# Last block of a conditioned residual chain: another order of W1's terms, x3T made from the transposed normalized values, and extra TensorE products

## The chip, the cores and the metric

The kernel runs on one core of a Trainium2 chip. The metric is the device time of one execution in microseconds (us), the median of three runs. One further execution was recorded by the hardware profiler; the profile and the trace are of that one. Engines are named as in the profile: PE is TensorE, DVE is VectorE, ACT is ScalarE, POOL is GpSimd, and SP is SyncE, whose queue starts most of the DMAs.

## The reference

The input is x, 128 sequences of 64 tokens with 256 features, and a condition vector of 128 numbers per sequence. Four layers are added to it, one after the other:

```python
x = x + L0(x, cond_512)        # attention with modulated projections
x = x + L1(x, cond_512)        # small adapter, weights made per sequence
x = x + L2(x, ids, cond_512, cond_64, fside)
x = x + L3(x, cond_512)        # linear layer, weights made per sequence
```

The change concerns the end of L2 and the beginning of L3. Cut to what matters:

```python
# L2: h, t, s are layer norms of x with gains and biases looked up by token ids,
#     m, n, r are x plus one vector per sequence; w = softmax(aw)
cat = concatenate([w0*h, w1*t, w2*m, w3*n, w4*r, w5*s])
y   = silu(cat @ W1 + b1) @ W2 + b2
L2  = (y - mean(y)) * rsqrt(var(y) + 1e-5) * g + be
# L3: U is made from mu per sequence, V is shared
weight, bias = U[:, :-1, :] @ V, U[:, -1, :] @ V
L3  = x @ weight + bias
```

## The kernel before, in words

The 8192 tokens are worked in 16 blocks of 512 tokens (8 sequences), a block in 4 tiles of 128 tokens. A prologue loads weights and derives tables that all blocks use. Each block runs `attention` (L0) and then `rest` (L1, L2, L3). Most values are kept with features on the partitions: x1T is x after L0, x2T after L1, x3T after L2, each 2 x 128 partitions by 512 tokens (index c for the half). For the layer norms x2T is turned to tokens on the partitions (x2, four tiles).

Steps of `rest` in order, with their lines:

- x2T is made by DVE at L1217, from the L1 products at L1204. PE transposes it (L1254), ACT copies the tiles out as x2 (L1257), and DVE takes their statistics (L451, L452).
- The normalized tiles xn (L1240) are multiplied by and added to gathered rows on POOL (L1265, L1271), which gives h; h is normalized again (L1240).
- xn and h are transposed (L1289) and copied out (L1292). Products with a one-hot matrix (L1298) give the gains by token, and DVE multiplies them in (L1307). The results are g, xnT and hnT.
- W1 is a sum of four terms in one PSUM bank for each half of the output (L1322): `w_t` by g, `w_x` by x2T, `w_s` by xnT, `w_h` by hnT. A last product (L1331) adds the biases. Each term takes two products of 128x512, in f32, and shows as four records a half. ACT and DVE make s2 of it (L1337, L1340).
- W2 (L1353) gives y by tile; DVE adds a bias (L1358) and takes the statistics mvy. POOL derives the factor ry and the offset nry (L456, L458, L1234, L1235; the power at L458 is the long one).
- ACT normalizes the four tiles (L1240). POOL multiplies each by the gain (L1364) and adds x2 (L1367): that is x3. PE transposes x3 (L1379); ACT adds the bias in the transposed layout (L1384): that is x3T.
- L3 is PE at L1396 (x3T by U), DVE at L1407 (zT), PE at L1422 (zT by V). DVE adds x3 (L1430) and SP stores (L1434), tile by tile.

The order of the instructions is not the order of this text. Every operation is recorded in a list with the buffers that it reads, writes or claims. The class `Plan` then orders all of them by a list schedule on the host, with its own costs for every engine (`pe(us, ...)`, `act`, `dve`, `pool`), its own idea of PE's clock, and a table of priorities, `TURNS`, one number for each operation of a block. There is one table for each of "prologue", "first", "second", "middle", "last but one" and "last"; where several operations can start at once on an engine, the lowest number goes first. Each engine then runs its instructions in this fixed order and waits with semaphores. Buffers are handed out by kind. There are four PSUM buffers of the kind "bank". There is one buffer of the kind "s2", which s2 and x3T take in turn. The first product of W1 claims it for its block, so that W1 of a block begins after the block before has read its x3T.

`early` is a constant of many columns that is loaded at the start; `lbe` is L2's bias `be` in it, one number per partition, and `lg` is the gain `g` repeated on all partitions.

Of the kernel before, what the change touches and what calls it, by code (L numbers as in the profile page):

```python
# [42 lines left out]
EARLY_WIDTHS = (B, 8, C, 2, 2, 1, C, C, C, 1, 6) + (C,) * 9  # L43
# [15 lines left out]
class Plan:  # L59
# [44 lines left out]
    def stream(self, t, work, full):  # L104

        now, left = t, work
        while left > 1e-9:
            n = int(now / self.WINDOW)
            speed = 1.0 if n and self.cells.get(n - 1, 0.0) >= self.BUSY else 0.5
            m = int((now + self.SEEN) / self.WINDOW)  # L110
            step = max(min((n + 1) * self.WINDOW, (m + 1) * self.WINDOW - self.SEEN) - now, 1e-6)
            step = min(step, left / speed)
            self.cells[m] = self.cells.get(m, 0.0) + step * speed * full / self.WINDOW
            left -= step * speed
            now += step
        return now - t

# [101 lines left out]
    -10633 41137 464 10909 -44878 -11608 -42604 -45090 10155 -44468  # L219
# [14 lines left out]
    -15193 -45201 -12582 9703 17987 22744 15597 -18168 17424 -28042 -41758 -7357 -451 25437 -8991 -12614 459 -11776  # L234
    29958 -7569 23567 -6641 13097 26814 -28106 7375 -575 12318 20069 -38198 23459 -38462 36836 27311 31943 -4776
    26854 -14776 2811 12753 3636 -20535 28655 16056 22892 -31515 6510 -3096 -41775 12301
# [14 lines left out]
    1457 -45077 -25320 -34934 -8032 -37786 -19094 -8437 5339 -12394 -20304 14994 3721 -11664 -7635 -27664 27176 20895  # L251
    26121 9336 -35791 -14043 -7673 8369 -42327 -31969 -25693 17291 2553 -36411 -3402 -15873 13422 7027 -32778 19435
    22712 -20010 12141 -39669 -37660 1149 -27222 -44023 37623 -37115 -18717 26495 3505 18710 -32292 -430 15236 18791
    21609 -17410 29738
# [13 lines left out]
    28780 21150 7584 9227 29132 5260 28987 31520 -2237 3828 8090 938 30118 3864 -4871 -7133 4057 30319 11418 -2268  # L268
    -597 -6095 7699 -2331 11788 11039 36273 619 1024 4669 34043 16725 5303 33221 -6438 31026 14080 11161 37456 23037
    11095 -11007 27922 -5110 11858 21714 35520 -1388 28909 27611 779 30000 -4851 23042  # L270
    """,
    "last but one": """
    -945 -5006 28741 3275 -555 -2679 4333 19756 13246 29462 3507 42603 5115 -1489 14772 22434 -2133 33481 31798 41815
    951 30003 36734 39833 31441 44287 36835 36712 48388 29816 33965 35152 6423 18014 27987 -10794 26523 6071 13375
    215 -9627 40936 -4357 6362 10572 4554 -7283 41533 17559 2437 32059 31798 -2882 16598 41191 820 4323 8748 36137
    -10897 4648 -575 -2079 4645 -3815 1256 27711 36689 35506 -1449 -434 19376 3801 26228 18811 24911 28300 -6303
    26981 -11699 25941 12883 26660 40398 20930 37525 4574 -10903 34299 29604 46591 6477 -4378 -5383 30451 28410 33294
    18120 33105 30216 -4508 44002 39404 3003 11400 29 3543 3766 -5799 -2138 811 18752 32082 3511 3445 11417 27797
    5708 -499 -3099 10586 -5165 8292 24437 31597 33482 -11432 5280 4641 43330 5970 12741 11648 -6313 39403 7099 3725
    -1194 -2199 33524 5684 -3093 -3282 30904 3501 1070 957 -1360 33574 5400 34372 27196 29366 -2640 -4017 6600 27342  # L280
    3755 1799 30520 32280 29029 46575 20997 32367 9369 29333 -3636 1757 5073 38 16950 4247 -3714 31630 -87 5434 33087
    13695 12804 -1538 27383 -6571 45385 6618 32455 18229 25530 13431 4352 28866 4197 42996 36274 28905 48852 20492
    25821 12505 -1402 -5360 3342 27949 30405 6793 33874 -4408 26737 -9042 5014 33335 43087 44838 12803 42849 4251
    28780 21150 7584 9227 29132 5260 28987 31520 -2237 3828 8090 938 30118 3864 -4871 -7133 4057 30319 11418 -2268
    -597 -6095 7699 -2331 11788 11039 36273 619 1024 4669 34043 16725 5303 33221 -6438 31026 14080 11161 37456 23037
    11095 -11007 27922 -5110 11858 21714 35520 -1388 28909 27611 779 30000 -4851 23042
    """,
    "last": """
    -945 -5006 28741 3275 -555 -2679 4333 19756 13246 29462 3507 42603 5115 -1489 14772 22434 -2133 33481 31798 41815
    951 30003 36734 39833 31441 44287 36835 36712 48388 29816 33965 35152 6423 18014 27987 -10794 26523 6071 13375  # L290
    215 -9627 40936 -4357 6362 10572 4554 -7283 41533 17559 2437 32059 31798 -2882 16598 41191 820 4323 8748 36137
    -10897 4648 -575 -2079 4645 -3815 1256 27711 36689 35506 -1449 -434 19376 3801 26228 18811 24911 28300 -6303
    26981 -11699 25941 12883 26660 40398 20930 37525 4574 -10903 34299 29604 46591 6477 -4378 -5383 30451 28410 33294
    18120 33105 30216 -4508 44002 39404 3003 11400 29 3543 3766 -5799 -2138 811 18752 32082 3511 3445 11417 27797
    5708 -499 -3099 10586 -5165 8292 24437 31597 33482 -11432 5280 4641 43330 5970 12741 11648 -6313 39403 7099 3725
    -1194 -2199 33524 5684 -3093 -3282 30904 3501 1070 957 -1360 33574 5400 34372 27196 29366 -2640 -4017 6600 27342
    3755 1799 30520 32280 29029 46575 20997 32367 9369 29333 -3636 1757 5073 38 16950 4247 -3714 31630 -87 5434 33087
    13695 12804 -1538 27383 -6571 45385 6618 32455 18229 25530 13431 4352 28866 4197 42996 36274 28905 48852 20492
    25821 12505 -1402 -5360 3342 27949 30405 6793 33874 -4408 26737 -9042 5014 33335 43087 44838 12803 42849 4251
    28780 21150 7584 9227 29132 5260 28987 31520 -2237 3828 8090 938 30118 3864 -4871 -7133 4057 30319 11418 -2268  # L300
    -597 -6095 7699 -2331 11788 11039 36273 619 1024 4669 34043 16725 5303 33221 -6438 31026 14080 11161 37456 23037
    11095 -11007 27922 -5110 11858 21714 35520 -1388 28909 27611 779 30000 -4851 23042
# [5 lines left out]
def resid_chain(ctx: ExitStack, tc: tile.TileContext, a: dict, out: bass.AP, nblk: int = NBLK):  # L308
# [104 lines left out]
    condT, tok8, kab, apart, hilo, rowid, oab, ob, lbe, bdl, aw, *small = columns("early", EARLY_WIDTHS)  # L413
# [15 lines left out]
    def pe(us, f, reads, writes, claims=(), full=1.0, mode=0):  # L429

        op("PE", us + 0.16, f, reads, writes, busy=us, claims=claims, full=full, mode=mode)

# [740 lines left out]
    def rest(blk, x1T, pw, oh, wdn, wup, tab, uT):  # L1173

        b0 = blk * NB

# [139 lines left out]
        for fc in range(C):  # L1316
            ps, th = Buf("bank"), Buf("tmp")
            for n, (w, src) in enumerate(((w_t, gs), (w_x, x2T), (w_s, xnT), (w_h, hnT))):
                for c in range(C):
                    pe(  # L1320
                        0.88,
                        lambda ps=ps, w=w, src=src, fc=fc, c=c, n=n: nc.tensor.matmul(  # L1322
                            ps.t, w.t[:, c, bass.ts(fc, 128)], src.t[:, c, :], start=(n == 0 and c == 0), stop=False
                        ),
                        [w, (src, c) if src is not x2T else src],
                        [ps],
                        [th, s2],
                    )
# [16 lines left out]
            )  # L1345
        mvy, ry, nry = Buf("mvy"), Buf("ry"), Buf("nry")
        x3 = [Buf("x3") for _ in range(NTILE)]
        for tl in range(NTILE):
            ps = Buf("bank")

            def second(ps=ps, tl=tl):
                for c in range(C):
                    nc.tensor.matmul(  # L1353
                        ps.t[:, :F], s2.t[:, c, bass.ts(tl, 128)], w2.t[:, c, :], start=(c == 0), stop=(c == C - 1)
                    )

            pe(0.88, second, [s2, w2], [ps], [x3[tl]])
            dve(256, lambda ps=ps, tl=tl: nc.vector.tensor_tensor(x3[tl].t, ps.t[:, :F], b2, ALU.add), [ps], [x3[tl]])  # L1358
            stats(x3[tl], mvy, tl)
        rstd(mvy, ry)  # L1360
        offset(mvy, ry, nry)
        for tl in range(NTILE):
            normalize(x3[tl], x3[tl], ry, nry, tl)
            pool(0.65, lambda tl=tl: nc.gpsimd.tensor_tensor(x3[tl].t, x3[tl].t, lg, ALU.mult), [x3[tl]], [x3[tl]])  # L1364
            pool(
                0.65,
                lambda tl=tl: nc.gpsimd.tensor_tensor(x3[tl].t, x3[tl].t, x2[tl].t, ALU.add),  # L1367
                [x3[tl], x2[tl]],
                [x3[tl]],
            )  # L1370
# [3 lines left out]
        for c in range(C):  # L1374
            ps = Buf("bank")

            def turn(ps=ps, c=c):
                for tl in range(NTILE):
                    nc.tensor.transpose(ps.t[:, bass.ts(tl, 128)], x3[tl].t[:, bass.ts(c, 128)], ident)  # L1379

            pe(0.5, turn, x3, [ps], [x3T])
# [66 lines left out]
def _layouts(i):  # L1448
# [32 lines left out]
    for n in ("mem", "noi", "res"):  # L1481
# [49 lines left out]
        + [columns(int_be)]  # L1531
# [28 lines left out]
```

## Time and profile before

| | value |
|---|---|
| runs | 897.14, 897.73, 900.79 us; median 897.73 |
| profiled execution | 896.84 us, its span 895.1 us |
| granted TensorE clock, mean | 0.984 |
| PE busy | 824.6 us (92% of the span) |
| DVE, ACT, POOL busy | 635.5, 446.8, 608.0 us |
| last block: x2T ready | 843.7 us |
| last block: first and last record of W1 | 854.22, 870.6 us |
| last block: nry ready | 878.4 us |
| last block: last addition of L1430 ends | 891.6 us |

The span goes from the first to the last instruction of the profiled execution; what lies around it makes the rest of its time. A chain of waits is followed back from the last instruction, at each step to what released it. Buffers that share memory show under the name of the memory in the trace: "uu", "p" and "bank" stand for several of the names above, so an operation is found by its line.

### The profile page before, as it was taken

Reading aid. Unit: us, or ns where it says so; the run is one execution under the profiler, and the core shown is the slowest. Engines: PE = TensorE matmul, PEld = TensorE weight load, DVE = VectorE, ACT = ScalarE, POOL = GpSimd, SP = SyncE. Lnnn points to the kernel's source line nnn. Section 1 sums busy time; section 2 is a strip of 40 time slices with the busy share of each in tenths; the row PEclk is TensorE's granted clock in tenths of the full one; section 3 lists DMA queues with packets and bytes.
Section 4 is the critical chain, followed back from the end, with each engine's and each line's share of the span. In section 5 each row is a group of like instructions: output and inputs, shape, how many; then the busy total and the mean of one; then the engine's idle time right before and its main releaser. Section 6 shows DMA issues by size and latency. Waiting matters only on the chain.

```text
span 895.1 us, 23962 instructions
## 1 busy us (share of the span) xinstructions
PE 824.6 (92%) x9752; PEld 534.3 (60%) x9752; DVE 635.5 (71%) x1363; ACT 446.8 (50%) x825; POOL 608.0 (68%) x826
## 2 busy tenths in 40 slices
PE   5769999999999999999999999999999999999783
PEld 3548746556665756666566657566665666564442
DVE  2779867868685868777786858787777868585532
ACT  1454453555464655545554645555455556464321
POOL 4464683949687795959495876959594968754423
PEclk9889999999999999999999999999999999999996
DMA  8768742223424232322333332333323322101000
GB/s 252 202 155 239 247 132 76 71 82 108 116 84 122 67 118 81 109 81 76 113 96 117 85 119 70 119 81 94 95 73 116 96 85 83 49 15 59 1 24 25
DMA packets 62575, 90.24 MB, mean 101 GB/s; under 512 B 6328, under 2 KB 46200, under 8 KB 62464
## 3 DMA queue, kind: packets, MB, share of 16 engines
q1 hardware_dynamic: 57344, 71.92, 28.1%
q0 software_dynamic: 5120, 16.78, 5.9%
q8 instruction: 77, 1.26, 0.6%
q14 instruction: 34, 0.28, 0.1%
HBM read 75.44 MB, written 13.24 MB: 99 GB/s over the span
## 4 chain that ended last, share of the span: by engine, by line
PE 44%; POOL 26%; DVE 13%; issue 6%; ACT 6%; DMA 3%; SPq 1%; POOLq 0%; DVEq 0%; ACTq 0%
PE bank L1322 15%; PE sc L1053 4%; DVE mt L1062 4%; PE bank L964 3%; PE bank L1353 3%; PE bank L1128 3%; PE bank L997 3%; POOL kxe L1011 2%; POOL wdn L938 2%; POOL uu L1271 2%; DVE st L451 2%; POOL xsT L907 2%; POOL uu L1265 2%; ACT uu L1240 2%; POOL uu L1364 1%
## 5 line engine op out<-in xcount | busy, mean ns | idle before, releaser
L1117 ACT ACTIVATE e<-sc 128x1024 f32<-128x1024 f32 x128 | 125.9, 1022 | 79.5 <-PE sc L1103 79.5
L1062 DVE TENSOR_REDUCE mt<-sc 128x8 f32<-128x1024 f32 x128 | 151.8, 1205 | 11.8 <-PE sc L1053 8.8
L1147 POOL TENSOR_TENSOR att<-ao,rz 128x256 f32<-128x256 f32 x45 | 28.1, 626 | 71.0 <-DVE rz L1144 66.8
L1307 DVE TENSOR_TENSOR uu<-uu,bank 128x512 f32<-128x512 f32 x96 | 63.8, 680 | 15.5 <-PE bank L1298 14.3
L997 PE MATMUL bank<-wk,xsT 128*128 128x256 f32 x256 | 70.1, 409 | 1.0 <-POOL xsT L907 1.0
L1322 PE MATMUL bank<-uu,w_s 128*128 128x512 f32 x128 | 66.9, 604 | 0.0
L1322 PE MATMUL bank<-uu,w_t 128*128 128x512 f32 x128 | 63.2, 604 | 2.2 <-DVE uu L1307 2.2
L1322 PE MATMUL bank<-x2T,w_x 128*128 128x512 f32 x128 | 64.4, 606 | 0.0
L1353 PE MATMUL bank<-w,uu 128*128 128x256 f32 x256 | 61.4, 383 | 1.0 <-DVE uu L1340 1.0
L456 POOL TENSOR_SCALAR ry<-mvy 128x4 f32<-128x4 f32 (+1 forms) x19 | 4.4, 232 | 85.3 <-DVE mvy L452 85.2
L964 PE MATMUL bank<-osT,wo 128*128 128x512 f32 x128 | 59.3, 604 | 0.5 <-DVE osT L1163 0.5
L997 PEld LDWEIGHTS bank<-wk,xsT 128*128 128x128 f32 x256 | 48.3, 200 | 19.3 <-issue 10.8
L1322 PE MATMUL bank<-uu,w_h 128*128 128x512 f32 x128 | 59.1, 597 | 0.6 <-DVE uu L1307 0.4
L1072 ACT COPY mt<-mt 128x16 f32<-128x16 f32 x64 | 13.1, 204 | 84.0 <-DVE mt L1062 83.9
L451 DVE BATCH_NORM_STATS2 st<-uu 128x6 f32<-128x256 f32 x119 | 48.3, 417 | 8.8 <-ACT uu L1257 4.7
L1011 POOL TENSOR_TENSOR kxe<-kxe,kbr 128x256 f32<-128x256 f32 x64 | 46.8, 731 | 8.7 <-DVE kxe L1005 6.3
L1353 PEld LDWEIGHTS bank<-w,uu 128*128 128x128 f32 x256 | 46.2, 190 | 8.3 <-DVE uu L1340 1.6
L938 POOL TENSOR_TENSOR wdn<-gdb,late 128x512 f32<-128x512 f32 x32 | 40.6, 1273 | 11.6 <-PE bank L1186 6.1
L1005 DVE TENSOR_TENSOR kxe<-bank,dmk 128x256 f32<-128x256 f32 x64 | 26.8, 419 | 29.9 <-PE bank L997 26.8
L922 POOL DMA_INDIRECT pw<-in_pw,idx x39 | 40.0, 1025 | 8.1 <-issue 7.2
L1140 DVE STREAM_TRANSPOSE ao<-bank 128x512 f32<-128x512 f32 x45 | 32.0, 711 | 18.0 <-PE bank L1128 18.0
L952 POOL TENSOR_TENSOR wup<-wup,ubb 128x512 f32<-128x512 f32 x32 | 40.6, 1269 | 3.5 <-DMA ubb<-ugub 1.3
(199 smaller groups left out, 2114.3 us busy)
## 6 DMA issues: line engine op xcount, KB each, us to landing
xT<-in_xT SPq DMA_DIRECT2D x32, 256.0 KB
gdb<-dgdb SPq DMA_DIRECT2D x16, 512.0 KB
ubb<-ugub SPq DMA_DIRECT2D x32, 256.0 KB
wup<-ugub SPq DMA_DIRECT2D x32, 256.0 KB
dmk<-demod_k SPq DMA_DIRECT2D x30, 256.0 KB
out_x<-uu SPq DMA_DIRECT2D x35, 128.0 KB
ud<-uu SPq DMA_DIRECT2D x8, 512.0 KB
uT<-ud SPq DMA_DIRECT2D x16, 256.0 KB
```

The costliest lines, as they stand in the source:

```text
L451: dve(256, lambda: nc.vector.bn_stats(st.t, x.t), [x], [st])
L922: lambda tl=tl, n=n: nc.gpsimd.indirect_dma_start(out=pw[tl].t, out_offset=None, in_=a["pw"], in_offset=bass.IndirectOffsetOnAxis(ap=idx[: ...
L938: lambda w=w, dp=dp: nc.gpsimd.tensor_tensor(w(), gdb.t[:, :, 0:64], dp, ALU.mult),
L952: pool(1.25, lambda w=w: nc.gpsimd.tensor_tensor(w(wup), w(wup), w(ubb), ALU.add), [wup, ubb], [wup])
L964: nc.tensor.matmul(ps.t, owT[:, c, bass.ts(oc, 128)], osT.t[:, c, :], start=(c == 0), stop=(c == C - 1))
L997: nc.tensor.matmul(ps.t[:, :F], xsT.t[:, c, bass.ts(tl, 128)], kwT[:, c, :], start=(c == 0), stop=(c == C - 1))
L1011: lambda: nc.gpsimd.tensor_tensor(kxe.t[:, :, 0:D], kxe.t[:, :, 0:D], heads(kinds["kbr"][0]), ALU.add),
L1062: lambda two=two: nc.vector.tensor_reduce(mt.t[:, two, 0:4], sc.t[:, two, :].rearrange("p q (g n) -> p q g n", g=4), AX.X, ALU.max),
L1117: lambda k=k: nc.scalar.activation(es[k].t, sc.t[:, 2 * k : 2 * k + 2, :], AF.Exp, scale=0.25),
L1307: lambda ps=ps, src=src, dst=dst, c=c: nc.vector.tensor_tensor(dst.t[:, c, :], src.t[:, c, :], ps.t, ALU.mult),
L1322: lambda ps=ps, w=w, src=src, fc=fc, c=c, n=n: nc.tensor.matmul(ps.t, w.t[:, c, bass.ts(fc, 128)], src.t[:, c, :], start=(n == 0 and c == ...
L1353: nc.tensor.matmul(ps.t[:, :F], s2.t[:, c, bass.ts(tl, 128)], w2.t[:, c, :], start=(c == 0), stop=(c == C - 1))
```

## The change

For the last block alone (`quick`), four things differ.

1. W1's terms come in another order: `w_x` by x2T first, then `w_t`, `w_s`, `w_h`.
2. ACT adds `lbe` to x2T in place, after everything else has read x2T. The normalized tiles go to buffers of their own, yn. PE transposes yn instead of x3, and one DVE operation makes x3T: the transposed yn, times the gain `lgT` (one number per partition, two new columns of `early`), plus x2T with its bias. POOL still makes x3 from yn for the final addition.
3. `keep` adds products that nobody reads. Each group starts with a product of four columns whose moving operand is a value just made (mvy, ry, nry, then yn of tiles 0, 1 and 2), and goes on with 4 (for the first three) or 3 products of the identity with itself, 128x128 in f32. They take a PSUM bank and PE's time. The plan books 0.12 us for each.
4. The priority tables "last but one" and "last" are new; in the others, places for the added operations are put in, and other blocks skip them (`skip`). "prologue" has six more numbers, for the six groups.

```diff
-EARLY_WIDTHS = (B, 8, C, 2, 2, 1, C, C, C, 1, 6) + (C,) * 9
+EARLY_WIDTHS = (B, 8, C, 2, 2, 1, C, C, C, C, 1, 6) + (C,) * 9
...
+    def skip(self, n):
+
+        self.noted[self.blk] += n
...
+    def keep(n, gate):
+
+
+        ps, blk = Buf("bank"), plan.blk
+        plan.blk = -1
+
+        def products():
+            nc.tensor.matmul(ps.t[:, :4], ident, gate[1](), start=True, stop=True)
+            for k in range(n):
+                nc.tensor.matmul(ps.t[:, bass.ts(k, 128)], ident, ident, start=True, stop=True)
+
+        pe(0.12 * n, products, [gate[0]], [ps])
+        plan.blk = blk
...
+        quick = blk == nblk - 1
...
-            for n, (w, src) in enumerate(((w_t, gs), (w_x, x2T), (w_s, xnT), (w_h, hnT))):
+            terms = (w_t, gs), (w_x, x2T), (w_s, xnT), (w_h, hnT)
+            if quick:
+                terms = terms[1], terms[0], *terms[2:]
+            for n, (w, src) in enumerate(terms):
...
+        if quick:
+            for c in range(C):
+                act(
+                    512,
+                    lambda c=c: nc.scalar.activation(x2T.t[:, c, :], x2T.t[:, c, :], AF.Identity, bias=lbe[:, c : c + 1]),
+                    [(x2T, c)],
+                    [(x2T, c)],
+                    more=0.093,
+                )
+        else:
+            plan.skip(C)
...
+        yn = [Buf("h") for _ in range(NTILE)] if quick else x3
...
+        if quick:
+            for value in (mvy, ry, nry):
+                keep(4, (value, lambda value=value: value.t.rearrange("p n k -> p (n k)")[:, :4] if value is mvy else value.t))
...
-            normalize(x3[tl], x3[tl], ry, nry, tl)
-            pool(0.65, lambda tl=tl: nc.gpsimd.tensor_tensor(x3[tl].t, x3[tl].t, lg, ALU.mult), [x3[tl]], [x3[tl]])
+            normalize(yn[tl], x3[tl], ry, nry, tl)
+            if quick and tl < NTILE - 1:
+                keep(3, (yn[tl], lambda tl=tl: yn[tl].t[:, :4]))
+            pool(0.65, lambda tl=tl: nc.gpsimd.tensor_tensor(x3[tl].t, yn[tl].t, lg, ALU.mult), [yn[tl]], [x3[tl]])
...
-                    nc.tensor.transpose(ps.t[:, bass.ts(tl, 128)], x3[tl].t[:, bass.ts(c, 128)], ident)
-
-            pe(0.5, turn, x3, [ps], [x3T])
+                    nc.tensor.transpose(ps.t[:, bass.ts(tl, 128)], yn[tl].t[:, bass.ts(c, 128)], ident)
+
+            pe(0.5, turn, yn, [ps], [x3T])
+            if quick:
+                dve(
+                    512,
+                    lambda ps=ps, c=c: nc.vector.scalar_tensor_tensor(
+                        x3T.t[:, c, :], ps.t, lgT[:, c : c + 1], x2T.t[:, c, :], ALU.mult, ALU.add
+                    ),
+                    [ps, (x2T, c)],
+                    [(x3T, c)],
+                )
+                continue
...
-        + [columns(int_be)]
+        + [columns(int_be), columns(i["L2_cond_int_g"])]
```

Of the tables, "middle", "first" and "second" keep their numbers. In "last but one" and "last" most numbers move by less than 100 and some single ones by thousands: in block 14, for example, the first of the two output products of L0 (L964; -5165 becomes 22471) and the transpose of the last x2 tile (L1254; 3501 becomes 31515); in block 15 two POOL operations that make h (L1265 of tile 0, L1271 of tile 1), which come earlier, and one of the two L1307 operations that make g, which comes later (4197 becomes 16940).

## The prediction

> **What bounds the kernel now.** I read the page's slices first, then the busy time in stretches, then the chain of waits, then the order of instructions near the end. The slices (each 22.4 us) say where a change to the last block can act at all:
>
> ```profile
> PE   5769999999999999999999999999999999999783
> PEclk9889999999999999999999999999999999999996
> ```
>
> TensorE is at nine tenths for thirty-four slices: there it is the bound. It falls to 7, 8 and 3 in the last three, and only there does the granted clock fall. Before about 830 us nothing is to be had from a shorter tail; after it, the time is a chain of single operations. The stretches:
>
> ```profile
> 850.00:860.00 10.00, 7.87 (x26) 3.61 (x25) 5.04 (x14) 2.53 (x6) 6.15 (x11) 1.00 0.16 53
> 860.00:870.00 10.00, 9.57 (x31) 4.47 (x30) 2.06 (x3) 2.75 (x5) 0.00 (x0) 1.00 0.00 0
> 870.00:880.00 10.00, 4.35 (x18) 2.96 (x16) 4.31 (x13) 2.19 (x5) 2.58 (x6) 1.00 0.00 0
> ...
> 880.00:882.00 2.00, 0.00 (x0) 0.00 (x0) 0.00 (x0) 0.48 (x1) 2.00 (x4) 0.52 0.00 0
> ...
> 884.00:886.00 2.00, 1.80 (x8) 1.48 (x8) 0.00 (x0) 0.43 (x1) 0.57 (x1) 0.50 0.00 0
> 886.00:888.00 2.00, 1.59 (x34) 0.83 (x32) 0.00 (x0) 0.94 (x2) 0.00 (x0) 0.50 0.04 8
> ```
>
> The columns are length, then busy time of TensorE, its weight loads, VectorE, ScalarE and GpSimd, then the granted clock. Two limits follow one another: W1 on TensorE until 870.6, then, from 876, a chain in which TensorE does nothing, loses half its clock at 880, and does not regain it. The chain of waits gives the order (start, length, engine, output, line):
>
> ```profile
> 878.17 0.21 POOL nry L1235
> ...
> 878.41 0.61 ACT p L1240
> ...
> 883.89 0.69 POOL p L1367
> 884.58 0.04 issue
> 884.63 1.77 PE bank L1379 x7
> 886.40 0.02 issue
> 886.42 0.70 ACT uu L1384
> 887.12 0.04 issue
> 887.16 0.91 PE bank L1396 x24
> 888.07 0.02 issue
> 888.10 0.30 DVE zT L1407
> ```
>
> L1422 follows at 888.44. All eight POOL operations (L1364, L1367) stand between the normalization and the transposes. The four L1430 additions end at 891.60 and the span 3.5 us later, with the last stores.
>
> **The tail, part by part.** I count from T = 878.38, the end of nry; before, the last L1430 ends at T+13.22.
>
> *Transposes no longer wait for POOL.* They read yn, whose four ScalarE operations end at 880.48, T+2.1. POOL still makes x3 (8 x 0.68, ending at T+6.2 as before), but beside the L3 path; it is needed first at L1430. So if nothing else stood in front, the transposes would begin at T+2.1 instead of T+6.25.
>
> *But TensorE is in order, and the unread products stand in front.* Their price decides where the transposes begin. The nearest row is a 128-column f32 product of the prologue:
>
> ```profile
> 68.66 1.95 PE L814 MATMUL bank<-early,p 128*128 128x128 f32 x16
> ```
>
> A product is two records there (120 records for 60 products), and 16 records take 1.95 us: 0.107 each once under way, so 0.215 a product. The change books 0.12. Hence four products with their gated 4-column one (two records, about 0.05 each) are some 0.95 us, three are 0.71 (pipelined behind others). The mvy group fits the idle time: it starts at T-1.9 (mvy ends at 876.46) and is over at T-0.95. The ry group starts at T-0.2 (the power ends at 878.09), ends at T+0.75; nry T+1.7; the three yn groups T+2.4, T+3.1, T+3.85. yn[3] is long ready; the eight transposes run from T+3.85 to T+4.7. [...] the row is this very f32 shape, so I take it: T+3.85.
>
> *One VectorE operation for scale, bias and residual.* It replaces the ScalarE bias (L1384, 0.69). The same form, per-partition scalar with a PSUM and an SBUF operand, is L982, 0.75 us; L1340 with a constant takes 0.68. Two in a row: T+4.3 to 5.05 and 5.05 to 5.75. The first overlaps the second half of the transposes. No gain, no loss beyond 0.06.
>
> *The clock.* With the groups, TensorE's longest idle stretch before T+4.7 is 875.34 to 876.5, against 8.6 us before. At full clock block 14's own tail is the row: L1396 x24 from start to zT's start 0.61 (847.41 to 848.02), zT to L1422 0.35, L1422 to the first L1430 0.84, the four additions 1.42. So L1396 T+5.8 to 6.4, zT to 6.7, L1422 at 6.75, first addition at 7.6, last ends at **T+9.0**. Against 13.22 that is **4.2 us**: 2.4 from the earlier transposes, about 0.7 for the transposes and eviction, 0.3 from L1396, 0.9 from L1422. POOL's x3 (T+6.2) is 1.4 us early: that is its cover.
>
> [...] 1.80 of 2 us busy at 884 to 886, all transposes, and the clock stays at 0.50 through 892. [...] so I take full clock and keep 1.2 for the range.
>
> **W1 begins with x2T.** In the last block the order was w_t, w_x, w_s, w_h. x2T is there at 843.66, the scaled g only at 854.17:
>
> ```profile
> 854.22 3.70 PE L1322 MATMUL bank<-uu,w_t 128*128 128x512 f32 x8 [1.94 <-DVE uu L1307]
> ```
>
> Eight records of w_x are 8 x 0.43 = 3.44 us that can move ahead. Not at once: W1 claims the one s2 buffer, which block 14's x3T holds until its L1396 ends at 848.0. Between 848.0 and 854.2 TensorE is idle for 3.0 us (one-microsecond stretches: busy 0.63, 0.30, 0.88, 0.93, 0.29, 0), and another 1.1 us falls before the last h transposes and copies. Next late is h: its normalization starts at 858.91, transposes and copies follow, and VectorE's last h scaling can't end before about 863.9 (861.0 + 0.86 transposes + 0.6 copy + 0.6 second copy + 0.25 product + 0.7). Then eight w_h records and the table product: 863.3 + 3.44 + 0.22, near 867.1, against 870.64. The gain is **3.4 us**, the smaller of w_x's length and that 3.5. Ends: zero, if two PSUM banks held from 848 by W1's sums (of four) make the g and xn products queue for the other two; 4.7, if the h statistics also stop queuing behind L1307 on VectorE (853.5 to 856.2, the last POOL product being ready at 854.49). The numbers that order block 15 do lower one L1307, but I don't count on it.
>
> *The bias on x2T.* Two ScalarE operations (nearest L1384, 0.69 each) wait for the last w_x product and all x2 transposes. ScalarE is idle from 851.86 to 858.91, so 1.4 us hide there; if w_x's second half came after 858, they would stand before h's normalization in ScalarE's queue and cost up to 1.4. Nothing taken.
>
> *New orders for the last two blocks.* They move no work off any engine. Most values shift by under 100; the ones that jump are single operations, such as block 14's first output product (L964). I take zero, plus or minus 1.
>
> *The rest.* Two more columns in the early load (704 bytes a row for 696) lie in the prologue; the skipped numbers emit nothing. SP keeps the same four stores, in order of completion; no queue is moved past another.
>
> **Sum.** 895.1 - 3.4 - 4.2 = 887.5 us of span. The profiled execution was 896.84, 1.74 over its span, so 889.2 for it; the median of the runs, 897.73, lies 0.89 higher: **890.1 us**.
>
> **Rivals.** A: the products are cheaper than the row (or some fall elsewhere in TensorE's order). Transposes at T+2.13, VectorE to T+4.1, L1422 at T+5.05, last addition at T+7.3, with POOL's T+6.2 now the close second: 5.9 instead of 4.2, 888.4 us. For it: the planner's booking. Against: L814. B: W1's early start is eaten by banks and by h; only the tail gains: 893.5. For it: four banks, and TensorE at 9.57 of 10 between 860 and 870, which a different order alone doesn't shrink. Against: 3 us of idle time just ahead. C, the change not doing what it says: the clock drops all the same. Then the groups take twice as long, transposes T+8.1 to T+9.85, VectorE to 10.9, L1396 to 11.85, L1422 at 12.2, last addition T+15.4: 2.2 us lost, 3.4 won, 896.5. D, the slower side: block 14's output product slips so far in the new order that its W1 (4 x 3.44 + 0.4 = 14.2 us) lies behind 830, when block 15's attention is done. The gaps from 830 to 854 hold about 6.3; 7.9 go on the end, and block 14's eight POOL operations (5.4) then meet block 15's eight: 13.3 more, less 7.6, gives 903.4. It decides from a slip of 7.6 us on; 12.1 to be measurable. Against: L964 is needed by everything after it, so the order itself suffers from such a slip.
>
> **Chances.** Forecast 0.62, A 0.18, B 0.10, C 0.05, D 0.05. A difference of 0.5% (4.5 us) is about what can be told from none. D is slower; C is the same; B lies just within 4.5 (half of it on either side); the forecast crosses it only where several ends meet. Faster 0.84, same 0.11, slower 0.05. Range: low 886.0 is 4.7 and 5.9 won and 1 by order (886.1); high 894.4 is W1 at 0.3 and the tail at 4.2 - 1.2.
>
> **What would show it.** Transposes of block 15 starting 3.9 us after nry with the clock at 1.00 (right), at 2.1 (A), at 0.50 (C). L1396 x24 at 0.54 us, L1422 near 0.71. W1's first record of block 15 about 848, its last table product near 867. The VectorE operation at 0.75. POOL's last L1367 before the first L1430. I'd be wrong altogether if block 15's x2T came more than 2 us away from 843.7.

## The result and the profile after

The changed kernel takes 892.71 us in the median of eight runs (891.2 to 894.98), the kernel before 897.62 (895.55 to 900.79). The ratio is 0.9946 with a 95% interval of 0.9926 to 0.9966: 4.9 us less (3.1 to 6.6). A second set of runs, with its own runs of the kernel before, gave 0.9948 (0.9930 to 0.9966). The forecast was 7.6 us less.

The profiled execution took 894.98 us, the slowest of the eight, with a span of 893.2. First TensorE and its clock in 40 slices, from the page of the kernel after:

```profile
PE   4669999999999999999999999999999999999886
PEclk9889999999999999999999999999999999999998
```

TensorE is busier at the end (8, 8, 6 for 7, 8, 3), and the last slice has clock 8 for 6. That looks like what was wanted. The shorter stretches of the same kernel say otherwise (length; busy time of TensorE, weight loads, VectorE, ScalarE, GpSimd; granted clock):

```profile
854.00:856.00 2.00, 1.71 (x3) 0.66 (x3) 1.81 (x6) 0.00 (x0) 1.46 (x3) 0.66 0.01 3
856.00:858.00 2.00, 2.00 (x4) 0.67 (x3) 0.13 (x1) 0.00 (x0) 1.62 (x4) 0.50 0.00 0
...
878.00:880.00 2.00, 2.00 (x13) 2.00 (x13) 0.00 (x0) 1.86 (x4) 1.29 (x3) 0.63 0.04 8
880.00:882.00 2.00, 2.00 (x12) 2.00 (x11) 0.00 (x0) 0.21 (x1) 2.00 (x4) 0.51 0.00 0
882.00:884.00 2.00, 2.00 (x19) 2.00 (x20) 0.00 (x0) 0.00 (x0) 1.92 (x4) 1.00 0.00 0
884.00:886.00 2.00, 1.59 (x18) 1.35 (x19) 0.84 (x2) 0.00 (x0) 0.45 (x1) 1.00 0.00 0
```

The clock is granted at 0.50 twice while TensorE is fully busy: from 854.6 to 858.1 (3.42 of 3.42 us), in W1's w_t, and from 878.5 to 882.0 (3.41 of 3.41 us), in the unread products themselves. The chain of waits from nry on (it ends at 878.10; L444 is the four-column product of a group, L446 are the others):

```profile
877.88 0.39 PE bank L444 x2
878.26 1.54 PE bank L446 x8
879.81 0.22 PE bank L444 x2
880.03 1.91 PE bank L446 x8
881.94 0.18 PE bank L444 x2
882.12 0.77 PE bank L446 x6
...
884.68 0.45 PE bank L1418 x4
885.13 0.03 issue
885.16 1.42 DVE uu L1424 x2
886.58 0.04 issue
886.62 0.59 PE bank L1445 x24
```

Before, eight POOL operations stood between nry and the transposes. Now five groups of products stand there, one behind the other, and the first transpose (L1418) starts 6.4 us after nry, later than the 5.6 of the kernel before (there one ran ahead and the other seven followed from 6.25 on). What remains of the gain comes behind them: L1445 at 0.59 us for 0.91, and the whole tail from nry to the last addition at 11.8 us for 13.2.

One caution on the spread. From block 2 on the two kernels run the same instructions until block 14. The step from one block's x2T to the next is 49.2 to 49.3 us in most blocks of the two profiles above, but 49.65 and 50.37 in many blocks of the profiles below, taken in other sets. That is several us over 13 blocks, as large as what is sought. Both profiles of the changed kernel also have a stretch of half clock near 155 us (0.50 from 154.9 to 158.3 in the first), and the block that it falls in takes 53.6 us for 52.2; the profile of e11 has it too and the others don't, so I don't count it to the change. So the ratios below are to the kernel before in the same set, and beside them I give stretches inside the last block. The names are: **W1** from the last block's x2T to W1's last table product; **nry** from x2T to the end of nry; **start** from nry to the first transpose of the tail; **tail** from nry to the end of the last addition; **end** from nry to the end of the span.

| kernel | ratio (95%) | W1 | nry | start | tail | end |
|---|---|---|---|---|---|---|
| before | 1 | 27.0 | 34.7 | 5.6 | 13.2 | 16.7 |
| changed | 0.9946 (0.9926 to 0.9966) | 25.4 | 33.6 | 6.4 | 11.8 | 15.1 |
| changed again (e5) | 0.9948 (0.9930 to 0.9966) | 23.7 | 31.9 | 6.4 | 11.8 | 15.2 |
| no products (e1) | 0.9918 (0.9904 to 0.9933) | 23.7 | 31.9 | 0.7 | 8.45 | 12.5 |
| no products, again (e10) | 0.9940 (0.9921 to 0.9959) | 24.2 | 32.3 | 0.7 | 8.45 | 12.5 |
| mvy and ry groups only (e2) | 0.9908 (0.9894 to 0.9922) | 23.7 | 31.9 | 1.0 | 8.45 | 12.5 |
| no yn groups (e12) | 0.9923 (0.9903 to 0.9944) | 23.7 | 31.9 | 2.1 | 7.5 | 12.5 |
| groups moved (e9) | 0.9943 (0.9928 to 0.9958) | 23.7 | 31.9 | 0.7 | 7.8 | 12.5 |
| groups moved, again (e11) | 0.9929 (0.9909 to 0.9948) | 23.7 | 31.9 | 0.7 | 7.8 | 12.5 |
| products doubled (e6) | 0.9982 (0.9972 to 0.9993) | 23.7 | 31.9 | 8.6 | 14.0 | 17.3 |
| old order of terms (e3) | 0.9972 (0.9961 to 0.9983) | 29.0 | 36.8 | 4.8 | 10.1 | 13.5 |
| old priority numbers (e4) | 0.9950 (0.9934 to 0.9967) | 24.8 | 33.0 | 4.8 | 10.2 | 13.5 |
| new x3T alone (e7) | 0.9943 (0.9923 to 0.9963) | 27.4 | 35.2 | 0.7 | 8.4 | 12.5 |
| new order of terms alone (e8) | 0.9967 (0.9958 to 0.9976) | 28.3 | 36.4 | 5.6 | 12.9 | 16.3 |

Within W1 and nry, stretches of half clock are counted in: about 3.4 us of it in the changed kernel's first profile (its second has none), about 10 in that of e3, about 10 in that of e8, about 7 in that of e7; in e10 such a stretch ended just as x2T was there.

The last column limits what the tail can bring. Seven of the profiles have tails from 7.5 to 8.45 us, and all seven end 12.45 to 12.46 us after nry. What ends last there is GpSimd. Behind its last operation (L1406) it closes the program with an instruction called DRAIN, which takes 6.08 us in the trace, begins beside that operation and ends 11.66 to 11.68 us after nry. SyncE, with the stores, is through before it. In e12, where nry ends at 880.03:

```profile
885.66 0.72 POOL L1406 TENSOR_TENSOR uu<-uu,p 128x256 f32<-128x256 f32 x1
...
L1605 SPq DRAIN  x3: 7/7/7, 890.0 to 892.0; - x3
L1605 POOLq DRAIN  x3: 45/102/6077, 885.6 to 892.2; - x3
L1605 POOLq EVENT_SEMAPHORE  x4: 17/17/17, 891.7 to 892.4; - x4
```

(The last three lines give the count, then shortest, median and longest duration in ns, then first and last start.) The first DRAIN of SyncE is at 890.0; GpSimd's first step after its long DRAIN is at 891.7. In e3, where the tail is longer, SyncE is through 2.6 us after the last addition. From these numbers I estimate that a tail shorter than about 9.1 us (11.7 less 2.6) brings nothing more.

### The profile page after: what moved, and what is told of

It reads as the page before. It is cut to its first block, busy times and chain, and to the rows that moved or that the text cites. A ratio compares the mean times of both kernels' runs of the same rounds, so it can differ in the third digit from the quotient of the medians.

```text
span 893.2 us, 24076 instructions
## 1 busy us (share of the span) xinstructions
PE 830.2 (93%) x9806; PEld 539.8 (60%) x9806; DVE 638.4 (71%) x1365; ACT 446.9 (50%) x825; POOL 608.0 (68%) x826
## 4 chain that ended last, share of the span: by engine, by line
PE 54%; POOL 18%; DVE 13%; ACT 6%; issue 5%; DMA 3%; SPq 0%; DVEq 0%; ACTq 0%; POOLq 0%
PE bank L1344 19%; PE sc L1071 4%; PE bank L982 4%; PE bank L1387 4%; PE bank L1015 4%; PE bank L1146 4%; DVE mt L1080 3%; POOL wdn L956 2%; PE sc L1121 2%; POOL kxe L1029 2%; PE bank L1058 2%; PE bank L1176 2%; POOL uu L1290 2%; PE bank L1317 1%; POOL xsT L925 1%
## 5 line engine op out<-in xcount | busy, mean ns | idle before, releaser
L1135 ACT ACTIVATE e<-sc 128x1024 f32<-128x1024 f32 x128 | 125.9, 1023 | 78.3 <-PE sc L1121 78.3
L1344 PE MATMUL bank<-uu,w_t 128*128 128x512 f32 x128 | 65.0, 618 | 0.5 <-DVE uu L1326 0.5
L1103 ACT ACTIVATE mX<-bank,early 128x128 bf16<-128x128 f32 x64 | 23.6, 369 | 38.3 <-PE bank L1096 38.3
```

Source lines behind the costliest of these rows:

```text
L1135: lambda k=k: nc.scalar.activation(es[k].t, sc.t[:, 2 * k : 2 * k + 2, :], AF.Exp, scale=0.25),
```

## The experiments

My theory after the profile was that the unread products cost more than the clock they hold: they are first in TensorE's order. The rival was that they pay, and that something else, W1 or the new orders, had not brought what was forecast.

**No products (e1).** Both uses of `keep` are left out.

```diff
-        if quick:
+        if False:
             for value in (mvy, ry, nry):
...
-            if quick and tl < NTILE - 1:
+            if False and tl < NTILE - 1:
                 keep(3, (yn[tl], lambda tl=tl: yn[tl].t[:, :4]))
```

> The changed kernel without any of the six groups of unread products. Theory (the products stand in TensorE's order before the transposes and cost more than the clock they hold): the transposes of the last block begin about 2.1 us after nry instead of 6.3 as in the changed kernel's profile, run at half clock, and the last addition ends about 8.6 us after nry instead of 11.8; some 890.5 us, no slower than the changed kernel's 892.7. Rival (the products pay): the tail at half clock costs 1.2 us more than at full and the time is 894 or above.

Ratio 0.9918. The first transpose starts 0.7 us after nry, when yn of tile 0 is there; the tail is 8.45 us, against 8.6 expected. Its stretches show that the clock was half all the way:

```profile
882.00:884.00 2.00, 1.42 (x3) 0.55 (x3) 0.00 (x0) 1.97 (x4) 1.43 (x3) 0.50 0.00 0
884.00:886.00 2.00, 1.76 (x14) 1.13 (x13) 1.36 (x2) 0.00 (x0) 2.00 (x3) 0.50 0.00 0
```

At half clock and with nothing in front it is 3.35 us shorter than the tail of the changed kernel with its products, and the end is 2.65 us earlier. The rival falls. The time is 7.4 us below the kernel before (6.0 to 8.7); e10, the same kernel in another set, gives 5.4 (3.7 to 7.1).

**Two groups (e2).** Those behind nry and yn are left out.

```diff
-            for value in (mvy, ry, nry):
+            for value in (mvy, ry):
...
-            if quick and tl < NTILE - 1:
+            if False and tl < NTILE - 1:
```

> Only the groups behind mvy and ry are kept; those behind nry and the three yn are gone. Theory: transposes about 2.1 us after nry; with the clock full the last addition ends 7.4 us after nry, with a dropped clock 8.6; 889.5 to 890.5 us, the fastest of these four. Rival (without the later groups the clock always falls and that decides): no better than the version without any group.

Ratio 0.9908, not distinguishable from e1. The clock was full up to about 1.3 us after nry, then fell to 0.50 (at 883.4); the tail is 8.45 as without any group. In this profile two groups cost nothing and held nothing.

**Old order of the terms (e3).**

```diff
-            if quick:
-                terms = terms[1], terms[0], *terms[2:]
```

> The changed kernel with W1's terms in the old order in the last block (w_t first). If the new order is worth what was forecast, 3.4 us: 896. If it is worth the 0.3 us that nry is earlier in the changed kernel's profile, because the clock falls during w_t: 893. TensorE's clock between 850 and 860 would then stay at 1.00 here.

Ratio 0.9972, against 0.9948 with the new order: some 2.2 us, between the two expectations, though the two intervals still touch. That the clock would stay full here was wrong. It stayed low for ten us (length 4.00, columns as above):

```profile
854.00:858.00 4.00, 3.66 (x11) 1.87 (x11) 1.59 (x5) 2.74 (x6) 3.84 (x6) 0.56 0.30 102
858.00:862.00 4.00, 3.66 (x5) 1.15 (x5) 2.95 (x8) 0.00 (x0) 2.39 (x6) 0.50 0.00 0
862.00:866.00 4.00, 4.00 (x8) 1.68 (x7) 0.00 (x0) 2.07 (x4) 0.97 (x2) 0.66 0.00 0
```

So the fall of the clock in W1 doesn't come with the new order alone; the old one has it too, in some executions. What the profile does tell is the price of the products at full clock: here the clock fell only at the very end of the tail (0.50 from 895.4), the first transpose is 4.8 us after nry and the tail is 10.1.

**Old priority numbers (e4).** In both tables the old numbers are back, with two inserted for the added operations.

```diff
     "last but one": """
-    -945 -5006 28741 3292 -555 -2679 4333
+    -945 -5006 28741 3275 -555 -2679 4333
...
     "last": """
-    -918 -4932 28785 3332 -569 37576 95
+    -945 -5006 28741 3275 -555 -2679 4333
...
```

> The changed kernel with the old priority numbers for the last two blocks. If the new orders are worth nothing: 892.7. If they cost the 0.8 us by which x2T of the last block is later in the changed kernel's profile: 891.9 and x2T near 843.5. If they are what brings h's statistics forward on VectorE (h's normalization 0.8 us earlier): 893.5 to 894.5.

Ratio 0.9950, as with the new ones. From x2T of block 14 to x2T of block 15 it is 45.3 us, as in the kernel before; with the new numbers 46.3. So the new orders do make x2T 1.0 us later. From there to nry it is 33.0 for 31.9. The sum is 78.3 against 78.2: given and taken back. The tail, at full clock, is 10.2.

**The changed kernel again (e5),** without an edit.

> The changed kernel once more, as the ground for the others on this chip. Some 4.9 us (0.55%) below the kernel before; the spread between its runs 3 to 4 us. Theory of the clock: wherever this profile has no stretch of half clock before the tail, the last block's W1 and W2 (x2T to nry) take 31.9 us, with one such stretch 33.6; the tail from nry to the last addition takes 10.1 at full clock and up to 11.8.

Ratio 0.9948. The profile has no half clock in W1, and x2T to nry is 31.9 as expected. In the tail the clock fell again inside the products, 1.0 us after nry (0.50 from 886.2 to 889.6): first transpose at 6.4, tail 11.8, as in the first profile. In both profiles of this kernel the products ran at half clock for one stretch of 3.4 us.

**Products doubled (e6).** Eight and six instead of four and three, written round the same bank.

```diff
-                keep(4, (value, ...
+                keep(8, (value, ...
...
-                keep(3, (yn[tl], ...
+                keep(6, (yn[tl], ...
```

> The changed kernel with twice the number of products in each group (8 and 6 for 4 and 3). Theory (they stand before the transposes at 0.215 us each): the ry and nry groups cost 0.86 more each, the yn groups 0.64 each, 3.6 in all; the transposes begin 8.4 us after nry at full clock for 4.8, the last addition ends at 13.7, and the time is 3 to 4 us above the changed kernel's. Rival (products run in idle time): no change of more than 1 us.

Ratio 0.9982: about 3 us above the changed kernel. At full clock the transposes begin 8.6 us after nry and the tail is 14.0 (8.4 and 13.7 expected). The chain of this kernel shows why, each group right behind the other:

```profile
888.28 0.12 PE bank L444 x2
888.40 1.89 PE bank L446 x16
890.29 0.12 PE bank L444 x2
890.41 1.44 PE bank L446 x12
```

Sixteen records in 1.89 and twelve in 1.44 are 0.12 us a record, 0.24 a product. Every product behind ry, nry and yn is on the path.

**The new way to x3T alone (e7).** No products, old order of terms, old priority numbers: the edits of e1, e3 and e4 together.

```diff
-        if quick:
+        if False:
             for value in (mvy, ry, nry):
...
-            if quick:
-                terms = terms[1], terms[0], *terms[2:]
```

> Only the new way to x3T: old order of W1's terms, old priority numbers, no products. Theory: the tail is 8.5 us at half clock for 13.2, so 4.8 us (0.53%) below the kernel before, as much as the whole change brings. Rival (the tail needs the products' clock to gain): 3 us or less.

Ratio 0.9943, 5.1 us less than before (3.3 to 7.0), and the tail is 8.4 at half clock. This part alone brings as much as the whole change. Its end, 12.5 for 16.7, says 4.2 us.

**The order of terms alone (e8).** Old way to x3T, old numbers, no products.

```diff
-        quick = blk == nblk - 1
+        quick = False
...
-            if quick:
+            if blk == nblk - 1:
                 terms = terms[1], terms[0], *terms[2:]
```

> Only the new order of W1's terms in the last block: old way to x3T, old priority numbers, no products. Theory: from x2T to nry 33.0 us for 34.7 (W1's end 2.2 earlier, W2 0.4 longer), the tail 13.2 as before; 1.7 us (0.2%) below the kernel before. The forecast's 3.4 would be 0.4%.

Ratio 0.9967: 3.0 us less (2.2 to 3.8), more than the 1.7 of the theory and close to the 3.4 of the forecast. Its profile can't settle the size: the execution took 904.15 us, the slowest of nineteen, with half clock for some ten us of W1 (0.50 from 851.6 to 861.8), and its W1 of 28.3 is longer than that of the kernel before.

**Groups moved (e9).** Six products behind the last tile's mvy, two behind ry, three behind the first half of x3T (while VectorE makes the second), none behind nry and yn; all are written round the same bank.

```diff
-            for value in (mvy, ry, nry):
-                keep(4, (value, ...
+            keep(6, (mvy, lambda: mvy.t.rearrange("p n k -> p (n k)")[:, 4:8]))
+            keep(2, (ry, lambda: ry.t))
...
+                if c == 0:
+                    keep(3, ((x3T, 0), lambda: x3T.t[:, 0, :4]))
```

> The changed kernel with the groups only where TensorE has nothing to do: six products behind the last tile's mvy, two behind ry, three behind the first half of x3T, none behind nry and yn. Theory: the transposes begin within 1.1 us of nry; the last addition ends 7.4 to 7.6 us after nry if the clock holds, 8.5 if it falls; 2.6 to 3.5 us below the changed kernel (ratio to before some 0.991). Rival (the groups can't hold the clock in so little time): no better than the version without any group, 0.992.

The clock held through the tail (1.00 until 894.2), which is 7.8 us, 0.6 less than without groups. But both kernels end 12.46 us after nry, so this 0.6 could not reach the time: GpSimd's DRAIN ends last in both. The ratio, 0.9943, is higher than expected, and its 22 runs spread from 894.8 to 905.5. So two of the kernels were run once more, in one set.

**No products, and groups moved, again (e10, e11),** the kernels of e1 and e9.

> The changed kernel without any group of products, beside the two others of this chip. Theory: the tail from nry to the last addition 8.4 us at half clock; 0.992 of the kernel before.

> The changed kernel with the groups where TensorE has nothing to do (behind the last tile's mvy, ry, and the first half of x3T). Theory: tail 7.8 us, so 0.6 us less than without any group: 0.991 to 0.992 of the kernel before. Rival: the time is that of the version without groups or above it, because the held clock doesn't pay in most executions.

Ratios 0.9940 and 0.9929; medians 897.65 and 896.35. The tails repeat to within 0.02 us (8.45 and 7.80). The end is 12.45 in both. In the whole time the difference, 1.3 us, is inside the intervals.

**No groups behind yn (e12).** Those behind mvy, ry and nry stay. It is one edit:

```diff
-            if quick and tl < NTILE - 1:
+            if False and tl < NTILE - 1:
                 keep(3, (yn[tl], lambda tl=tl: yn[tl].t[:, :4]))
```

> The changed kernel without the three groups behind yn; those behind mvy, ry and nry stay. Theory: at full clock the nry group ends about 2.0 us after nry, when the last yn is ready, and the last addition at 7.5 to 8.2; if the clock falls at the ry group, transposes from 3.9 on and 9.5 to 10. Between the changed kernel and the version without groups: 0.992 to 0.994.

Ratio 0.9923, and the lowest median of the three in this set, 895.3. The chain, with nry ending at 880.03:

```profile
880.19 1.00 PE bank L446 x8
881.18 0.12 PE bank L444 x2
881.31 1.00 PE bank L446 x8
882.30 0.45 PE bank L1418 x4
882.75 0.02 issue
882.78 1.42 DVE uu L1424 x2
884.20 0.04 issue
884.24 0.59 PE bank L1445 x24
```

The nry group ends just when the last yn is there; the transposes start at 2.1 and the tail is 7.5 us, the shortest of all. As a time it is not shown to beat e1, e2 or e11, and from nry to the end of the span it doesn't: 12.46, as theirs. Its ratio is 0.0023 below the changed kernel's and the intervals overlap; the case against the yn groups is the end: 12.5 us here, 13.5 with the groups where the clock held (e3, e4), 15.1 and 15.2 in the two profiles of the changed kernel.

## Why the prediction was right and wrong

The direction was right, and 892.7 lies in the range. The gain was 4.9 us for 7.6. Rival B's figure, 893.5, is nearer than the forecast's 890.1, but its account is not what happened: it has all the gain in the tail, and in the runs W1's part was there too, and the tail's was smaller. By the prediction's steps:

*The transposes no longer wait for POOL.* Right. Freed of everything in front (e1, e7), the tail is 8.4 us for 13.2. POOL's x3 ends 6.3 us after nry, about as it was put, 4 us before the changed kernel's first L1479. But the sum took the end of the span to stay 3.5 us behind the last addition. That holds down to a tail of about 9.1 us, by the estimate above; below it POOL's DRAIN ends the program. The forecast's T+9.0 was just there. Rival A's T+7.3 could not have brought its 5.9: from nry to the end no kernel won more than 4.2 (16.7 to 12.5).

*The products stand in front, until T+3.85.* The mechanism was right, the size was not. I took 0.107 us a record "once under way" from a row of 16 records in 1.95 us. That was an estimate: one record of the row takes 0.275 us, which puts their starts 0.112 apart, and divided through it is 0.122. At full clock the groups run at 0.12 to 0.13, so a product costs about 0.25, not 0.215. The row divided through was near. The ry group's four-column pair shows 0.38 us in the chain of e4, the others 0.12, for the 0.1 taken. At full clock the transposes start at T+4.8 (e3, e4), 0.95 later than forecast. The tail is 10.1 for 9.0: a gain of 3.1 for 4.2 (from nry to the end 13.5 for 16.7, so 3.2).

*The clock.* "I take full clock" failed, in both profiles of the changed kernel, and by another way than the one for which I kept 1.2 us in the range (0.3 at L1396 and 0.9 at L1422, an estimate from the tails of block 14 and of the last block before). I let the mvy group fill the idle time before ry. Its gate reads the first four columns of mvy, which are tiles 0 and 1, so it started 1.3 us before the statistics were finished (876.19) and ended with them:

```profile
874.89 0.29 PE L444 MATMUL bank<-mvy,ident 128*128 128x4 f32 x2
875.04 1.14 PE L446 MATMUL bank<-ident 128*128 128x128 f32 x8
...
877.88 0.27 PE L444 MATMUL bank<-ry,ident 128*128 128x4 f32 x1 [1.70 <-POOL ry L476]
```

The idle time of 1.7 us before the ry group stayed, the clock fell to 0.50 at 878.54, and what was left of the ry group and the nry group ran at half speed (1.91 us for the 1.00 of e12). Then the products, not the L3 path, paid for the half clock: T+6.4, tail 11.8, a gain of 1.4. That is rival C's mechanism, for one stretch of 3.4 us instead of the whole tail. The idle time alone doesn't decide it: e3, e4 and e12 have the same 1.70 us and kept the clock (1.00 until 895.4, 889.4 and 888.7). Rival A's place, transposes at T+2.1 and last addition at T+7.3, was reached only by taking the yn groups out (2.1 and 7.5). The row of transposes at half clock (884 to 886) doesn't show what transposes do to the clock in general: in e7 it went from 0.50 to 1.00 right behind 3.42 us filled with them (last section). And in the slices of the kernel before the clock is low in the second and third too (8), not only at the end; nothing rests on it.

*The VectorE operation.* Two took 1.42 us, 0.71 each, for 0.75 and 0.70.

*W1 begins with x2T.* The mechanism was right, the 3.4 us too large: in the traces 1.7 to 1.8 are left at nry. Its first w_x record starts at 846.16, not at about 848, because block 14 read its x3T earlier. At full clock x2T to W1's end is 23.7 for 27.0, which is 3.2 and looks right; but with the new orders x2T itself is 1.0 later, and with the old ones W1 is 24.8, 2.2 less. Then W2 gives back 0.4: before, the two halves of W1 ended 2.8 us apart, and two W2 records ran before the second half of s2 was there; now they end 1.1 apart (868.85 and 869.92), and all sixteen wait for the second. That makes the 1.7 to 1.8 at nry. In whole times the step was worth 3.0 alone (e8) and 2.2 within the change (e3). How much of the difference is the clock in W1, which falls in some executions with either order, I could not settle.

*The bias on x2T.* Nearly right: it ran at 851.23 to 852.55, and the chain has 0.6 us of it ahead of the transposes of xn.

*The new orders.* Taken as nothing, and nothing they are in sum, +1.0 and -1.1. Rival D's slip was one of 1.0 us, far from the 7.6 from which it decides, and x2T at 844.5 is inside the 2 us that were set as its sign.

Put together, at full clock, 1.8 up to nry and 3.2 behind it make 5.0, and 4.9 was measured. That it comes out so close is partly luck, since neither kernel is always at full clock: with 1.6 behind nry, as in the first profile of the changed kernel, where the clock fell, the sum is 3.4. Without the products 1.8 and 4.2 make 6.0, between the 7.4 of e1 and the 5.4 of e10. So the unread products took back about 1 us where the clock held and about 2.7 where it fell, and they could win nothing, because below a tail of about 9.1 us another engine ends the program.

## What to carry to other kernels

Work that is added to hold an engine's clock goes into that engine's order like any other (here five groups in a row ahead of the first transpose, which began 6.4 us after nry): give it only idle time that ends on something late, and count what it costs when the clock falls all the same, because then it takes longer itself (1.91 us for 1.00, the nry group). Price it from a row divided through to its end, and look at what its gate really waits for. Follow the chain to the end of the program, not to the last useful operation: here tails of 7.5, 7.8 and 8.45 us all ended together, 12.5 us after nry, because GpSimd's closing instruction had become the last. When a change has several parts, run the plain structural one by itself; here the new way to x3T alone brought as much as everything together.

## What the runs showed of the hardware that was not expected

- The granted clock of the profile after changed at distances that are multiples of 3.41 us. The stretches of half clock begin at 854.64, 878.54 and 888.78, and the first two end at 858.06 and 881.95: from one change to the next it is 3.42, 20.48, 3.41 and 6.83 us, which is 1, 6, 1 and 2 times 3.41.
- At half clock, a busy TensorE did not always get the full clock back at once. In e3 it was busy 3.66 of 4 us at 854 to 858 and again at 858 to 862, with 0.56 and 0.50 granted; behind a stretch filled with W1's wide products (4.00 of 4 us busy at 862 to 866) the clock was back at 864.7.
- Once the clock came back behind transposes alone. In e7, at half clock, one stretch of 3.42 us holds sixteen transposes and no other product (eight to x2, eight to block 14's x3T), and the clock is full right behind it:

```profile
848.80:852.22 3.42, 3.42 (x16) 3.18 (x16) 1.97 (x8) 2.15 (x5) 1.07 (x4) 0.50 0.02 5
852.22:855.63 3.41, 1.77 (x42) 0.99 (x42) 0.97 (x4) 2.60 (x6) 2.62 (x5) 1.00 0.00 0
```

  In the kernel before it did not come back behind the transposes of the tail (884 to 886, 1.80 of 2 us busy, 0.50); of the 3.42 us from 883.50 TensorE was busy for 2.60 there, and the clock stayed at 0.50 behind them.
- What keeps the clock was not shown. The changed kernel went from 1.00 to 0.50 after the 3.41 us from 851.23, with TensorE busy for 2.12 us. If steps of 3.41 us are counted back from the falls of e12 (888.71) and e4 (889.41), e12 kept 1.00 after those from 881.88, with 2.25, and e4 after those from 841.62, with 1.65. So busy time alone doesn't order these three.
- GpSimd's long DRAIN at the end ended 5.32 us after its last operation in the kernel before (884.57 to 889.89) and in the changed kernel (884.44 to 889.76), and 5.3 us after it in e12 (886.38 to 891.7).
